# Two graph convolutions, part by products with the matrix of edges, part by gathered rows

## The chip, the cores and the metric

The kernel runs on one core of one Trainium2 chip. The metric is the device time of one execution in microseconds (us); the time of a kernel is the median of its runs. The engines are named as in the profile: PE is the matrix unit (PEld its weight load), DVE the vector engine, ACT the scalar engine, POOL the engine that issues gathers and scatters (indirect DMAs), SP the queue that issues the plain DMAs.

## The reference, cut to what matters

A network of eight layers works on 3125 nodes with 256 features and 53125 edges. The fifth layer is a pair of plain graph convolutions; the change concerns it.

```
deg  = segment_sum(1, dst);  dinv = rsqrt(deg);  norm = dinv[src] * dinv[dst]
def gcn_conv(h, W, b):
    m = (h @ W)[src] * norm[:, None]
    return segment_sum(m, dst) + b
x1 = gcn_conv(x, W1, b1)
x1 = x1 / max(norm of each row of x1, 1e-12)
x2 = gcn_conv(x1, W2, b2)
out = x2 + x
```

The edge list has one self loop per node besides (`src` and `dst` already hold one, the convolution adds a second). What costs is the sum over the edges of each node: row n of the result is the sum of the table's rows `src` over the edges that end in n.

## The kernel before, in words

**The nodes.** The nodes are put in order of falling number of edges and cut into `NT` = 25 groups of 128. Group g has `KS[g]` slots for edges, from 41 in group 0 to 10 in group 24; the last eight groups have 15, 15, 14, 14, 13, 12, 11 and 10 slots, 104 of the `TOT` = 453 in all. `OFF[g]` is where group g begins among them. A slot holds the number of the node at the other end of an edge (`recs_i[:, k, 0]`); slots beyond a node's edges are dead (`live` is 0 there, `pen` very negative).

**The layers that gather.** Most layers fetch one row per slot and node: `gather` (L1079) is one indirect DMA on POOL, 128 rows from a table in DRAM into one column of a tile; `scatter` (L1083) is the reverse. The relational convolution (`plain_sum`, 2153 to 2890 us in the profile) gathers 453 such columns of 128 x 256 numbers, four to a tile `gt`, and adds them on PE with an identity matrix (L1705).

**The matrix of edges.** The pair of plain convolutions doesn't gather. In the layer before it (a gate layer with experts, `gates_by_slots`, 2890 to 3790 us) the kernel builds, beside that layer's own gathers and matmuls, a matrix of edge counts `adj` in DRAM: for each group g a block of 128 x 25 x 128 numbers in bf16 (800 KB), which tells how many edges run from each of the 3200 nodes to each node of the group. `edge_places` works out the places, writes them to `slots_d`, and `edge_columns` loads them back in two DMAs for each group (L1774, L1777). `one_hots` makes two bf16 tiles on DVE (L1800), `edge_blocks` multiplies them on PE (L1813), ACT copies the product out (L1817, L1821), and SP stores it (L2494). `beside_gates` is a generator of 31 pieces: piece i makes the one-hots of group i - 3, the block of group i - 4, and a part of the experts' matmuls (`hidden` L2438, `back` L2452, `biased` L2459). The gate layer's loop `in_turns` takes pieces at a pace that follows its count of gathers. In that layer the order of the instructions on each engine is the order in which the program writes them.

**A convolution.** `edge_sum(table, tail)` runs twice. The nodes' rows times W, scaled by dinv, lie in a DRAM table (`tables[0]`, then `tables[1]`) and, for the self loop, in `own`. First five loads (L2556, 640 KB each) bring the table in, and ACT and DVE split it into three bf16 parts whose sum is the f32 value (`F12` and `F3_`, L2558 and L2559). Then, for each group: SP loads the group's block of `adj` (L2563, three buffers), PE multiplies it with the 25 tiles of the table, a matmul of 512 columns and one of 256 for each (L2566, L2569), so 50 matmuls a group into `acc` (two buffers in PSUM); DVE adds the halves and `own` (L2575, L2576); and a tail runs. `tail1` scales, and after every fifth group (`BATCH` = 5) normalises five groups, turns them on PE (L1454), multiplies by the second W (`to_table`, L2588), and scatters them into `tables[1]` (L1083), one step of that generator in each later turn of the group loop. `tail2` adds b2, the residual and the layer norm of the next layer, and the next layer's router matmul (L2643).

**What sets the order.** Here the program doesn't fix the order on each engine: a planner that works with its own costs for each instruction orders them when the kernel is built, by the program's order and by when it believes their inputs are there. It moves work that is ready ahead: in the profile the additions of b2 (L2628), which belong to the second convolution, run before the first.

Of the kernel before, what the change touches and what calls it, by code (L numbers as in the profile page):

```python
# [11 lines left out]
F32 = mybir.dt.float32  # L12
BF16 = mybir.dt.bfloat16
I32 = mybir.dt.int32
# [1040 lines left out]
DC = KS[0] + 3  # L1055
BATCH = 5
# [357 lines left out]
def quick(ctx: ExitStack, tc: tile.TileContext, a: dict, out: bass.AP, k):  # L1414
# [26 lines left out]
    def table_of(name, width, rows=NP + 1):  # L1441

        t = dram.tile([rows, width], F32, name=name)
        nc.sync.dma_start(t[NP : NP + 1, :], zero[:, :width])
        return t
# [266 lines left out]
    adj = dram.tile([NT, P, NT * P], BF16, name="adj")  # L1712
# [3 lines left out]
    for g in range(NT):  # L1716
        w = min(10, P // KS[g])
        n = -(-P // w)
        if at % P + n > P:
            at = -(-at // P) * P  # L1720
        TILES.append((w, n, at))
        at += n
    TB = -(-at // P)
    slots_d = dram.tile([2 * P * TOT], F32, name="slots_d")

    def slots_of(g):
        return slots_d[2 * P * OFF[g] : 2 * P * OFF[g + 1] if g + 1 < NT else 2 * P * TOT]

    t_at = q.tile([P, NT], F32, name="t_at")
    with tc.tile_pool(name="ep", bufs=1) as pool:  # L1730
        NJ = max(n for _, n, _ in TILES)
        firsts = pool.tile([P, NT, NJ], F32, name="ep_first")
        for g, (w, _, _) in enumerate(TILES):
            nc.gpsimd.iota(firsts[:, g, :], pattern=[[w, NJ]], base=w, channel_multiplier=0,
                           allow_small_or_imprecise_dtypes=True)
        j_f = pool.tile([P, 1], F32, name="ep_j")
        nc.gpsimd.iota(j_f, pattern=[[0, 1]], base=0, channel_multiplier=1, allow_small_or_imprecise_dtypes=True)
        past = pool.tile([P, NT, NJ], F32, name="ep_past")
        nc.vector.tensor_scalar(past, firsts, j_f, None, op0=ALU.is_le)
        t = t_at  # L1740
        nc.vector.tensor_reduce(t, past, AX.X, ALU.add)

        nc.vector.scalar_tensor_tensor(t, t, -1.0, firsts[:, :, 0], op0=ALU.mult, op1=ALU.mult)
        nc.vector.tensor_scalar(t, t, j_f, None, op0=ALU.add)

    def edge_places(pool):
# [12 lines left out]
        nc.vector.scalar_tensor_tensor(pb[:, 1, :], pen, -512.0 / BIG, pb[:, 1, :], op0=ALU.mult, op1=ALU.add)  # L1759
        for g in range(NT):  # L1760
            o = slice(OFF[g], OFF[g] + KS[g])
            nc.sync.dma_start(slots_of(g).rearrange("(s p k) -> p s k", s=2, p=P), pb[:, :, o])
# [650 lines left out]
    def beside_gates(pool, wp, psum):  # L2413
# [56 lines left out]
        for i in range(U + 3):  # L2470
# [6 lines left out]
            if 3 <= i < NT + 3:  # L2477
                hots[i - 3] = one_hots(pool, cols, columns, i - 3)
            g = i - 4
            products = iter(())  # L2480
            if 0 <= g < NT:
                As[g] = pool.tile([P, NT, P], BF16, name="em_a")
                products = edge_blocks(psum, g, *hots.pop(g), As[g])
# [9 lines left out]
            if 0 <= g - 1 < NT:  # L2493
                nc.sync.dma_start(adj[g - 1], As.pop(g - 1).rearrange("p b j -> p (b j)"))  # L2494
# [39 lines left out]
    with tc.tile_pool(name="ng", bufs=3) as gp, tc.tile_pool(name="ns", bufs=3) as sp, \  # L2534
# [10 lines left out]
        tables = [dram.tile([NP, D], F32, name=f"gcn{i}") for i in (1, 2)]  # L2545
# [4 lines left out]
        def edge_sum(table, tail):  # L2550
# [9 lines left out]
            tails = []  # L2560
            for g in range(NT):
# [3 lines left out]
                for b in range(NT):  # L2565
# [4 lines left out]
                                     skip_group_check=True)  # L2570
                for t in list(tails):
                    if next(t, None) is None:
                        tails.remove(t)
                s_ = sp.tile([P, D], F32, name="sum")
                nc.vector.tensor_add(s_, acc[:, 0, :], own[:, g, :])  # L2575
                nc.vector.tensor_add(s_, s_, acc[:, 1, :])  # L2576
# [20 lines left out]
        def tail1(g, acc):  # L2597
# [5 lines left out]
            sq = sp.tile([P, D], F32, name="sq")  # L2603
# [394 lines left out]
```

## Time and profile before

| what | us |
|---|---|
| median of 3 runs | 6321.4 (6282.28 to 6326.48) |
| the profiled execution, its own time | 6232.02 |
| its span | 6230.3 |
| gate layer, with the matrix of edges built beside it | about 2890 to 3790 |
| first convolution: first load of the table to its last scatter | 3903 to 4158 |
| second convolution: first load of the table to the last sum | 4159 to 4396 |

A view by stretches of time gives, for each stretch, how long each engine was busy and in brackets how many instructions it began, then the clock granted to PE (1.00 is full), the share of the 16 DMA engines and what they moved. A view by groups gives busy time and mean duration in ns of all instructions of a line, then the engine's idle time just before them and what ended it. "issue" means that the engine waited for nothing that the profile shows, "remote" that the releaser is not known. The mean PE clock over the span is 0.757.

### The profile page before, as it was taken

Reading aid. Unit: us, or ns where it says so; the run is one execution under the profiler, and the core shown is the slowest. Engines: PE = TensorE matmul, PEld = TensorE weight load, DVE = VectorE, ACT = ScalarE, POOL = GpSimd, SP = SyncE. Lnnn points to the kernel's source line nnn. Section 1 sums busy time; section 2 is a strip of 40 time slices with the busy share of each in tenths; the row PEclk is TensorE's granted clock in tenths of the full one; section 3 lists DMA queues with packets and bytes.
Section 4 is the critical chain, followed back from the end, with each engine's and each line's share of the span. In section 5 each row is a group of like instructions: output and inputs, shape, how many; then the busy total and the mean of one; then the engine's idle time right before and its main releaser. Section 6 shows DMA issues by size and latency. Waiting matters only on the chain. (4 is left out here: it accounts for less than half of the span.)

```text
span 6230.3 us, 45124 instructions
## 1 busy us (share of the span) xinstructions
PE 3790.6 (61%) x14119; PEld 2484.5 (40%) x14119; DVE 3125.4 (50%) x6023; ACT 1222.3 (20%) x2574; POOL 3127.8 (50%) x3044
## 2 busy tenths in 40 slices
PE   2345443455699854535396432889676788838882
PEld 1233332333455433423264221556343344436662
DVE  4588868898983345601164236333224677810001
ACT  1222222445622100000053221110121000012220
POOL 3677774677773266676467663010126666430004
PEclk9667666766799856756698666999656777869996
DMA  4534442333312233222252124332243333234442
GB/s 124 141 105 108 107 110 77 92 93 103 88 24 90 111 92 91 79 74 54 60 166 74 36 54 124 107 110 92 84 118 87 84 86 90 64 115 155 160 160 85
DMA packets 357953, 602.95 MB, mean 97 GB/s; under 512 B 109331, under 2 KB 254331, under 8 KB 354370
## 3 DMA queue, kind: packets, MB, share of 16 engines
q0 software_dynamic: 130800, 329.16, 20.1%
q1 hardware_dynamic: 207657, 251.79, 12.7%
q10 hardware_dynamic: 19238, 18.93, 1.0%
q8 instruction: 116, 1.90, 0.1%
q14 instruction: 142, 1.16, 0.1%
HBM read 458.77 MB, written 142.93 MB: 97 GB/s over the span
## 5 line engine op out<-in xcount | busy, mean ns | idle before, releaser
L1620 PE MATMUL acc<-wv,ident 128*128 128x256 f32 x2818 | 933.7, 492 | 611.9 <-ACT wv L1632 248.1
L1079 POOL DMA_INDIRECT gt<-T,recs x906 | 1011.3, 1116 | 341.4 <-issue 237.5
L1620 PEld LDWEIGHTS acc<-wv,ident 128*128 128x128 f32 x2818 | 666.6, 248 | 878.3 <-ACT wv L1632 280.1
L1079 POOL DMA_INDIRECT gt<-TA,recs x453 | 458.5, 1012 | 237.1 <-issue 124.8
L1079 POOL DMA_INDIRECT gt<-gm,recs x428 | 466.1, 1089 | 205.0 <-issue 126.8
L1079 POOL DMA_INDIRECT gt<-rel,relz x453 | 443.4, 979 | 203.6 <-issue 127.7
L1705 PE MATMUL acc<-gt,ident 128*128 128x256 f32 x906 | 321.9, 487 | 203.6 <-issue 155.7
L2566 PE MATMUL acc<-XNT,adj_g 128*128 128x512 bf16 x1250 | 416.4, 384 | 44.5 <-ACT XNT L2558 44.5
L2797 PE MATMUL e_ps<-EW,att 32*128 32x512 f32 (+7 forms) x466 | 300.5, 772 | 131.8 <-ACT att L2787 90.4
L1672 ACT ACTIVATE m<-m 128x1024 f32<-128x1024 f32 (+2 forms) x258 | 256.4, 994 | 614.0 <-DVE m L1671 378.2
L1671 DVE TENSOR_TENSOR m<-gt,R 128x1028 f32<-128x1028 f32 (+4 forms) x258 | 297.0, 1151 | 103.0 <-DMA gt<-T,recs 99.4
L1079 POOL DMA_INDIRECT y<-top_out,top_pos x50 | 48.0, 959 | 595.2 <-issue 594.9
L2569 PE MATMUL acc<-F,adj_g 128*128 128x256 bf16 x1250 | 342.8, 275 | 5.4 <-DVE F L2559 5.4
L1705 PEld LDWEIGHTS acc<-gt,ident 128*128 128x128 f32 x906 | 206.2, 240 | 301.7 <-issue 186.2
L1677 DVE TENSOR_TENSOR m<-m,att 128x1024 f32<-128x1024 f32 (+2 forms) x258 | 294.1, 1140 | 43.4 <-issue 28.1
L2909 PE MATMUL fh_ps<-xt,w 128*128 128x256 f32 x1024 | 265.1, 397 | 76.2 <-ACT ht L2911 75.4
L1678 DVE TENSOR_REDUCE L<-m 128x4 f32<-128x1024 f32 (+4 forms) x258 | 294.3, 1141 | 10.0 <-DVE m L1677 2.0
L1634 DVE TENSOR_TENSOR wv<-gt,L 128x1024 f32<-128x1024 f32 (+3 forms) x252 | 285.1, 1136 | 16.9 <-remote 12.8
L2438 PE MATMUL x_ps<-XNT,x_w 128*128 128x512 f32 (+1 forms) x448 | 213.2, 608 | 104.1 <-ACT x_h L2440 53.2
L2909 PEld LDWEIGHTS fh_ps<-xt,w 128*128 128x128 f32 x1024 | 186.6, 192 | 149.6 <-ACT ht L2911 127.8
L2452 PE MATMUL x_o<-x_w,x_h 128*128 128x256 f32 x800 | 204.5, 401 | 35.8 <-issue 32.9
L2921 PE MATMUL fo_ps<-w,ht 128*128 128x256 f32 x1024 | 226.3, 379 | 0.0
(557 smaller groups left out, 6417.9 us busy)
## 6 DMA issues: line engine op xcount, KB each, us to landing
w<-in_L_ffn_W_dram SPq DMA_DIRECT2D x64, 1024.0 KB
adj_g<-adj SPq DMA_DIRECT2D x50, 800.0 KB
adj<-em_a SPq DMA_DIRECT2D x25, 800.0 KB
gt<-T,recs POOLq DMA_INDIRECT x906
y<-each_d SPq DMA_DIRECT2D x25, 512.0 KB
each_d<-x_y SPq DMA_DIRECT2D x24, 512.0 KB
R<-rr SPq DMA_DIRECT2D x25, 388.0 KB
top_in<-zeros SPq DMA_DIRECT2D x8, 1024.0 KB
```

The source lines that it names most:

```text
L1079: return nc.gpsimd.indirect_dma_start(out=out_, out_offset=None, in_=table, in_offset=index(idx))
L1620: nc.tensor.matmul(acc, ident, wv[:, s, :], start=(c + s == 0), stop=(c + s == K - 1))
L1634: nc.vector.tensor_mul(wv[:, :n, :].rearrange("p s (h c) -> p s h c", h=H), t[:, :n, :D].rearrange("p s (h c) -> p s h c", h=H), L[:, c : ...
L1671: nc.vector.tensor_add(m[:, :n, :], st[g].tiles[c][:, :n, :], st[g].R[:, 1:2, :].to_broadcast([P, n, W]))
L1672: nc.scalar.activation(m[:, :n, :D], m[:, :n, :D], AF.Abs)
L1677: nc.vector.tensor_mul(m[:, :n, :D], m[:, :n, :D], att[:, None, :].to_broadcast([P, n, D]))
L1678: nc.vector.tensor_reduce(L, m[:, :n, :D].rearrange("p s (h c) -> p s h c", h=H), AX.X, ALU.add)
L1705: nc.tensor.matmul(accs[g], ident, t[:, s, :], start=False, stop=(last and s == n - 1))
L2566: nc.tensor.matmul(acc.rearrange("p s d -> p (s d)"), A[:, b, :], F12[:, b, :, :].rearrange("p s d -> p (s d)"), start=(b == 0), stop=Fals ...
L2569: nc.tensor.matmul(acc[:, 0, :], A[:, b, :], F3_[:, b, :], start=False, stop=(b == NT - 1), skip_group_check=True)
L2797: nc.tensor.matmul(e_ps[:, :z, :].rearrange("p s d -> p (s d)"), att, EW[: att.shape[0], s0 : s0 + z, :].rearrange("p s d -> p (s d)"), st ...
L2909: nc.tensor.matmul(ps[:, i, :], ld[j][1][:, c, (f_ + i) * P : (f_ + i + 1) * P], xt[j][:, c, :], start=(c == 0), stop=(c == KD - 1))
```

## The change

The matrix of edges is made and used for the first `GD` = 17 groups only. The other eight get their edge sums by gathers:

- `adj`, `slots_d`, `t_at`, `firsts` and `past` shrink to 17 groups; `edge_places`, `edge_columns`, `one_hots`, `edge_blocks` and the stores of `adj` run for 17.
- The two tables get one more row, of zeros, and a tile of indices `zi` points every dead slot of the last eight groups to it.
- In `edge_sum` a generator `gathered` gives, for each chunk of at most four slots (29 chunks, 104 gathers), the gathers into a tile `gt` (128 x 4 x 256, three buffers), one DVE reduction over the slots, and one DVE addition into `own`. Two chunks are taken after the products of each group. The gathers' order is groups 20 to 24, then 17 to 19.
- The groups' order is 0 to 9, 20 to 24, 10 to 19, so that a batch of five is either wholly products, wholly gathered, or (15 to 19) two of products and three gathered. A gathered group has no `acc`; its sum is `own` itself.
- The buffers of `sum` and `sq` go from three to two.

```diff
+GD = 17
-    adj = dram.tile([NT, P, NT * P], BF16, name="adj")
+    adj = dram.tile([GD, P, NT * P], BF16, name="adj")
-    for g in range(NT):
+    for g in range(GD):
         w = min(10, P // KS[g])
...
-    slots_d = dram.tile([2 * P * TOT], F32, name="slots_d")
+    slots_d = dram.tile([2 * P * OFF[GD]], F32, name="slots_d")
...
-        for g in range(NT):
+        for g in range(GD):
             o = slice(OFF[g], OFF[g] + KS[g])
             nc.sync.dma_start(slots_of(g).rearrange("(s p k) -> p s k", s=2, p=P), pb[:, :, o])
...
-            if 3 <= i < NT + 3:
+            if 3 <= i < GD + 3:
                 hots[i - 3] = one_hots(pool, cols, columns, i - 3)
             g = i - 4
             products = iter(())
-            if 0 <= g < NT:
+            if 0 <= g < GD:
                 As[g] = pool.tile([P, NT, P], BF16, name="em_a")
                 products = edge_blocks(psum, g, *hots.pop(g), As[g])
...
-            if 0 <= g - 1 < NT:
+            if 0 <= g - 1 < GD:
                 nc.sync.dma_start(adj[g - 1], As.pop(g - 1).rearrange("p b j -> p (b j)"))
...
-        tables = [dram.tile([NP, D], F32, name=f"gcn{i}") for i in (1, 2)]
+        tables = [table_of(f"gcn{i}", D) for i in (1, 2)]
+
+        o = OFF[GD]
+        z = wp.tile([P, TOT - o], F32, name="z_f")
+        nc.vector.tensor_scalar(z, recs_i[:, o:, 0], float(-NP), None, op0=ALU.add)
+        nc.vector.tensor_mul(z, z, live[:, o:])
+        zi = wp.tile([P, TOT - o], I32, name="z_i")
+        nc.vector.tensor_scalar(zi, z, float(NP), None, op0=ALU.add)
...
-            tails = []
-            for g in range(NT):
+            tails, ready = [], set()
+
+            def gathered():
+
+                for g in [*range(NT - BATCH, NT), *range(GD, NT - BATCH)]:
+                    for c, n in chunks(g):
+                        t = gp.tile([P, C4, D], F32, name="gt", bufs=3)
+                        for i in range(n):
+                            k_ = OFF[g] - OFF[GD] + c + i
+                            gather(nc, t[:, i, :], table, zi[:, k_ : k_ + 1])
+                        part = sp.tile([P, D], F32, name="g_part", bufs=2)
+                        nc.vector.tensor_reduce(part, t[:, :n, :].rearrange("p s d -> p d s"), AX.X, ALU.add)
+                        nc.vector.tensor_add(own[:, g, :], own[:, g, :], part)
+                        if c + n == KS[g]:
+                            ready.add(g)
+                        yield 0
+
+            def products(g):
                 A = gp.tile([P, NT, P], BF16, name="adj_g")
                 nc.sync.dma_start(A.rearrange("p b j -> p (b j)"), adj[g])
                 acc = psum.tile([P, 2, D], F32, name="acc", bufs=2)
...
+                return acc
+
+            beside = gathered()
+            for g in [*range(2 * BATCH), *range(NT - BATCH, NT), *range(2 * BATCH, NT - BATCH)]:
+                if g < GD:
+                    acc = products(g)
+                    for _ in range(2):
+                        next(beside, None)
+                while g >= GD and g not in ready:
+                    next(beside)
                 for t in list(tails):
                     if next(t, None) is None:
                         tails.remove(t)
-                s_ = sp.tile([P, D], F32, name="sum")
-                nc.vector.tensor_add(s_, acc[:, 0, :], own[:, g, :])
-                nc.vector.tensor_add(s_, s_, acc[:, 1, :])
+                s_ = own[:, g, :]
+                if g < GD:
+                    s_ = sp.tile([P, D], F32, name="sum", bufs=2)
+                    nc.vector.tensor_add(s_, acc[:, 0, :], own[:, g, :])
+                    nc.vector.tensor_add(s_, s_, acc[:, 1, :])
                 t = tail(g, s_)
...
-            sq = sp.tile([P, D], F32, name="sq")
+            sq = sp.tile([P, D], F32, name="sq", bufs=2)
```

## The prediction

> **What bounds the kernel now.** I read the stages first: the view by stretches over the two convolutions, from the first sums to the last.
>
> ```profile
> 3927.00:4144.00 217.00, 213.87 (x1305) 133.67 (x1304) 65.24 (x168) 16.24 (x41) 18.55 (x17) 1.00 0.31 104
> 4183.00:4396.00 213.00, 209.38 (x1310) 129.03 (x1308) 63.41 (x191) 10.01 (x26) 0.00 (x0) 0.99 0.26 87
> ```
>
> The columns are PE, PEld, DVE, ACT, POOL, then PE clock, DMA share, GB/s. PE works without a break at full clock, DVE for 30%, POOL hardly at all. So here PE is the bound, and each group's products are on the path. Their price comes from the timeline of DVE, by the distance between sums.
>
> ```profile
> 3954.21 0.42 DVE L2575 TENSOR_TENSOR sum<-acc,own 128x256 f32<-128x256 f32 x1 [5.81 <-PE acc L2569]
> 3962.33 0.42 DVE L2575 TENSOR_TENSOR sum<-acc,own 128x256 f32<-128x256 f32 x1 [5.81 <-PE acc L2569]
> ...
> 4051.39 0.42 DVE L2575 TENSOR_TENSOR sum<-acc,own 128x256 f32<-128x256 f32 x1 [6.90 <-PE acc L2569]
> 4060.60 0.42 DVE L2575 TENSOR_TENSOR sum<-acc,own 128x256 f32<-128x256 f32 x1 [3.95 <-PE acc L2569]
> ```
>
> A group costs 8.12 us on PE (50 matmuls); with a step of a tail (4 matmuls of L2588, 2 of L1454) 9.21. DVE waits some 6 us of each for PE.
>
> The new work is gathers beside matmuls, so I looked where the kernel does that already: the relational convolution, first the instructions that touch the tile `gt`, then a burst of gathers by stretches of 5 us.
>
> ```profile
> L1079 POOL DMA_INDIRECT gt<-rel,relz x450: 943/949/2987, 2153.2 to 2867.1; - x150
> ```
>
> ```profile
> 2284.00:2289.00 5.00, 5.00 (x24) 4.43 (x23) 1.42 (x5) 0.00 (x0) 3.78 (x5) 0.99 0.38 105
> 2289.00:2294.00 5.00, 5.00 (x25) 4.37 (x23) 4.76 (x11) 0.00 (x0) 3.78 (x5) 1.00 0.38 104
> 2294.00:2299.00 5.00, 1.86 (x5) 0.62 (x3) 4.83 (x10) 0.00 (x0) 3.78 (x5) 0.88 0.35 105
> ...
> 2304.00:2309.00 5.00, 1.17 (x2) 0.57 (x2) 2.52 (x6) 0.00 (x0) 3.78 (x5) 0.50 0.37 104
> 2309.00:2314.00 5.00, 1.17 (x2) 0.47 (x2) 0.00 (x0) 0.00 (x0) 3.78 (x5) 0.50 0.37 105
> ```
>
> This is the finding on which the forecast turns. A gather takes 0.95 us of POOL, and the timeline shows 0.30 between two: 1.25 us. The burst starts at 2281; PE begins 24 matmuls in 5 us, then, some 14 us into the burst, only 2, with its clock at 0.50, though DMA moves no more than before. It stays so until POOL stops. A second burst (from 2327) shows the same after 17 us. I call this the drag: POOL issues gathers without a pause for 14 to 17 us (I take 16, 13 gathers), and the other engines almost stop. When POOL pauses they come back, 3.5 us after the end of the last issue (2485.2 to 2488.7) or 5.5 (2535.7 to 2541.1). The profile gives no cause ("issue").
>
> The stage that builds the matrix of edges has the same, and waits:
>
> ```profile
> POOL gt L1079 <- DVE pen L2342: 67.6, 2, 34.6
> POOL own L1079 <- DVE L L2343: 53.8, 1, 53.8
> ```
>
> There POOL's gathers are the bound for most of the time, broken by waits for DVE, which has queued behind PE.
>
> **What the Trainium skill says.** "DMA: Bandwidth & Descriptors", section "Issuing engines are not separate DMA queues": DMAs from POOL and SP interleave on the same 16 engines. The trace agrees that they can: loads for `adj` and gathers together would be 98 GB/s (800 KB in 8.12 us) plus 105 GB/s, and the stretch 3800 to 3850 moved 276 at a share of 0.87; so transfers fit. "SBUF — State Buffer", section "Who interferes with whom": a tensor_reduce never contends with POOL on this chip, a DVE instruction with two SBUF inputs contends with what POOL reads there. In the trace gathers beside the one-hots (L1800, two SBUF inputs) stretch from 0.95 to 2.2 and 3.1 us. So the new reductions shouldn't slow the gathers; the one-hots taken away did. "TensorE: Matmul & The Clock Gate", part 1: after an idle window of about 3.4 us the array runs at half clock, and as long a busy time lifts it; the clock of 0.50 above agrees. No page describes the drag.
>
> **The change, part by part.**
>
> *Products removed.* 8 groups x 8.12 = 65.0 us of PE for each convolution; the tails of these groups stay. 17 x 8.12 + 25 x 1.09 = 165 stays of 230.
>
> *Gathers added.* 104 x 1.25 = 130 us of POOL for each convolution, beside 165 of PE. The first twelve (three tiles) can run while the table is loaded (9 us from the first load to the first matmul, over 20 to the last split): covered. Then two chunks a group: the first ten groups take 72 gathers, 7.2 each, 9.0 us, against 9.2 of PE. So without the drag they are just hidden; POOL hardly ever pauses, and the drag comes. Over two groups: 14.4 gathers, 18.0 us; PE has done 16.0 of its 18.4, 2.4 is left. POOL then stops, since its three tiles wait for reductions that stand on DVE behind the sum of the group PE hasn't finished. PE returns after 4, and needs 2.4 at full or 4.8 at half clock, say 3.4: 25.4 in place of 18.4, a loss of 7.0. First convolution: (72 - 12) / 14.4 = 4.2 such cycles, 29 us; its last 32 gathers share POOL with the scatters of `tail1`, before each of which POOL waits now (8.12 us each time, for ACT), and these pauses break the bursts: nothing. Second convolution: no scatters, 92 / 14.4 = 6.4 cycles, 45 us.
>
> *Reductions and additions on DVE.* 29 per convolution. The shape isn't in the trace. L1678 reduces 1024 numbers in 1.22 us; L2356, which reads with a stride as the new one will, takes 0.72 for about 350, so 2.1 for 1024 at most. With 0.42 for the addition two chunks cost 3.3 to 5.0 us a group, beside 2.6 that DVE does now (65.24 / 25): 7.6 at most of 9.2, hidden under PE. If PE's cover were gone it would be 48 to 73 us.
>
> *Ends.* Groups 17 to 19 come last with no products, so the last batch's scaling, square and reduction (0.48 + 0.42 + 0.42 each) no longer lie beside matmuls: 3 x 1.3 = 4, with a step of the earlier tails about 5 us for each convolution (0 to 12).
>
> *The matrix for 17 groups.* One-hots, 61 of 252 copies on ACT, 8 stores and 16 loads of `em_w` go. The first group concerned is met at 3389 us. From there to 3780 POOL issues for about 291 us, its gathers are stretched by one-hots of the groups removed by 3.4 + 3.1 + 4.2 + 3.6 + 3.9 = 18 us (excess over 0.95), and it waits 33 and 22 us for DVE, during which pieces take 15.4 us each (stores of `adj` at 3550.9, 3566.1, 3582.2), of which the 15 or 16 edge matmuls at 0.17 are 2.7: three pieces, 8 us. The 16 loads on SP (0.7 to 1.5 us each, up to 2960) may let PE start earlier: 5. Against it: the stretched gathers were pauses that ended the drag, and without them bursts are longer; I take off 11. Sum 20, between -15 and +45.
>
> *Nothing:* `z`, `zi`, the row of zeros, fewer stores of `slots_d`: a handful of small instructions beside the layer before, under 2 us if uncovered. `sum` and `sq` with two buffers: both are used up within 1.4 us on DVE itself.
>
> *Sum.* First convolution 65 - 29 - 5 = 31, second 65 - 45 - 5 = 15, gate layer 20: 66. The profiled execution, 6232 (its span 6230.3 and 1.7 around it), would become 6166. It lay 1.4% below the median of the runs shown, so I take the difference from the median: 6321.4 - 66 = 6255.
>
> **Rivals.**
>
> *The gathers are hidden.* Waits of POOL on DVE, or stretched gathers, break the bursts before 16 us, and the drag never sets in. For it: in the gate layer's stretch 3150 to 3250, where one-hots break the bursts, PE is busy for 89 of 100 us. Against it: 14.4 gathers in 18 us leave no pause. Gain 2 x (65 - 5) + 20 = 140: 6181.
>
> *The planner runs the gathers ahead.* If by its costs a gather is cheaper than it is, more chunks' reductions stand on DVE ahead of each sum than the two of the program. With three: 12 gathers, 15 us, and some 2 until the tiles are free again; 104 / 12 = 8.7 groups at 17 and 8.3 at 9.2 are 224 us, and with the ends nothing is gained: 20 - 10 = 10, 6311. For it: the additions of b2 show how far it moves work ahead.
>
> *Slower.* The same mechanism, past that point of three chunks a group: if all reductions stand ahead of the first sums, nothing on DVE holds POOL back, the burst lasts 130 us, and PE does 16 us of work in it, then comes back after 4 and does 149: 283 against 230. Two such are 2 x (53 + 5) - 20 = 96 lost: 6417. Against it: three tiles only, and the program's order.
>
> **How the numbers follow.** The likeliest case, drag in part, has 0.45, its own range 6205 to 6300 (drag after 14 or 17.5 us, gate layer at its bounds); hidden 0.2; three chunks ahead 0.2; slower 0.15. About 1% (63 us) is what a measurement of this kernel can tell from no change. Faster by more: a little over half of the first case, all of the second, a little of the third, 0.49. Slower: most of the fourth, 0.14. The same: 0.37. The range, 6165 to 6385, takes in the second case and leaves out most of the fourth.
>
> **What would show it.** Right: PE's instructions drop in stretches of 5 us after 13 gathers in a row, a period of two groups near 25 us in the second convolution, and the first gaining more than the second. Wrong: groups at 8.1 to 9.2 us throughout (hidden), or a run of more than 20 gathers with PE at x2 (slower). If the gate layer's end moves by more than 45 us either way, my account of that stage is wrong.

## The result, and the profile after

| | before | changed |
|---|---|---|
| median of 14 runs, us | 6306.22 (6269.32 to 6330.69) | 6347.26 (6308.49 to 6376.61) |
| profiled execution, span | 6230.3 | 6308.6 |
| first convolution, first split of the table to the next convolution's first split | 255.6 | 277.6 |
| of it, to the first sum | 27.5 | 52.8 |
| second convolution, first split to last sum | 231.0 | 249.4 |
| of it, to the first sum | 28.1 | 54.1 |
| gate layer, first gather of rows of `gm` to the last reduction | 860.6 | 859.6 |

The changed kernel takes 1.0069 times as long (95% interval 1.0048 to 1.0090), 0.7% more, where 1% less was forecast. The two profiles differ by 78 us, and 40 of them lie in the two convolutions. Most of the rest is 22 us ahead of the gate layer, where the change touches almost nothing, and 20 us behind the second convolution. Profiles of one kernel differ there by as much: the changed kernel begins its gate layer at 2903.7 us in one profile (e9) and at 2960.6 in another (e17), and from the last sum on the kernel before takes 1834.8 us here and 1848.3 in e12. So these 42 us aren't put down to the change. Line numbers of the changed kernel are 2 higher than before from L1057 to L1758, and 3 to 38 higher after that (L2575 became L2613).

The stretches of the convolutions, from first sums to last, answer to the two shown of before (217 us with PE busy for 213.87, 213 with 209.38).

```profile
3979.00:4070.00 91.00, 45.92 (x199) 22.00 (x204) 41.99 (x63) 0.21 (x1) 56.70 (x60) 0.68 0.38 113
4070.00:4175.00 105.00, 104.21 (x622) 66.65 (x633) 40.49 (x115) 11.24 (x32) 15.46 (x15) 1.00 0.31 107
4258.00:4352.00 94.00, 44.66 (x195) 20.89 (x200) 43.53 (x69) 0.21 (x1) 56.96 (x60) 0.67 0.38 111
4352.00:4453.00 101.00, 99.64 (x628) 63.00 (x640) 38.50 (x137) 5.61 (x18) 0.00 (x0) 1.00 0.22 74
```

Each convolution falls in two. While POOL gathers, PE is busy for half the time. Then no gathers are left, and PE runs the other groups at full clock with no gathers beside them. By the program's order the gathers were to lie beside 15 of the 17 groups; they lie beside the first six.

The reason is seen in the order in which DVE's instructions were built. Here r is a reduction of a chunk, f a split of the table (L2569), S the sum of a group:

```
first convolution   rfrfffrrrffffrrrfrfrrSSrrrrSrrrrSrrrrrSrrrrrSSSSSSSSSSSS
```

The program asks for two reductions a group. The planner put 11 of the 29 ahead of the first sum, none ahead of the second, 4 or 5 ahead of each of the next four, and several ahead of the splits, on which the first products wait. The timeline of DVE shows what that costs at the start:

```profile
3924.64 1.88 DVE L2581 TENSOR_REDUCE g_part<-gt 128x256 f32<-128x1024 f32 x1 [25.30 <-DMA gt<-gcn,z_i]
3926.45 1.48 DVE L2569 TENSOR_TENSOR F<-F,XNT 128x1280 f32<-128x1280 f32 x1
...
3930.60 1.89 DVE L2581 TENSOR_REDUCE g_part<-gt 128x256 f32<-128x1024 f32 x1 [2.34 <-DMA gt<-gcn,z_i]
3932.41 4.30 DVE L2569 TENSOR_TENSOR F<-F,XNT 128x1280 f32<-128x1280 f32 x3
...
3969.20 1.90 DVE L2581 TENSOR_REDUCE g_part<-gt 128x256 f32<-128x1024 f32 x1 [2.77 <-DMA gt<-gcn,z_i]
3977.44 1.88 DVE L2581 TENSOR_REDUCE g_part<-gt 128x256 f32<-128x1024 f32 x1 [6.34 <-DMA gt<-gcn,z_i]
3979.24 0.42 DVE L2613 TENSOR_TENSOR sum<-acc,own 128x256 f32<-128x256 f32 x1
```

A split stands behind a reduction that waits for its gathers, again and again. And the first sum stands behind the eleventh reduction. PE had finished both groups for which it has buffers at 3972.2, and stood still until the sums freed them:

```profile
3980.47 0.58 PE L2592 MATMUL acc<-XNT,adj_g 128*128 128x512 bf16 x1 [8.28 <-DVE sum L2613]
```

The drag of the prediction is there too: PE almost stops while POOL issues gathers. Below this is also called starving. By stretches of 5 us of the changed kernel (columns as before):

```profile
3985.00:3990.00 5.00, 5.00 (x30) 2.89 (x29) 3.85 (x5) 0.00 (x0) 3.78 (x5) 0.93 0.38 106
3990.00:3995.00 5.00, 0.99 (x5) 0.19 (x2) 1.69 (x2) 0.00 (x0) 3.78 (x5) 1.00 0.37 102
3995.00:4000.00 5.00, 0.96 (x2) 0.20 (x2) 0.63 (x1) 0.00 (x0) 3.78 (x5) 0.60 0.37 98
4000.00:4005.00 5.00, 0.95 (x2) 0.21 (x2) 0.00 (x0) 0.00 (x0) 3.07 (x4) 0.50 0.46 114
4005.00:4010.00 5.00, 2.35 (x6) 0.97 (x8) 0.44 (x2) 0.00 (x0) 0.00 (x0) 0.50 0.05 16
```

PE begins 2 matmuls in 5 us with no wait in its timeline but "issue". POOL's last issue ends at 4003.98, and the sum of PE's group starts at 4009.56, 5.6 us later. The gathers themselves went nearly as fast as thought (0.95 us in the median; the mean of 1.02 comes from those beside the splits, up to 2.5):

```profile
L1081 POOL DMA_INDIRECT gt<-gcn,z_i x208 | 211.5, 1017 | 101.3 <-issue 63.6 <-DVE g_part L2581 36.2 <-DMA gt<-gcn,z_i 1.2
```

In the gate layer two of POOL's waits are nearly those of before (61.4 for `pen` and 52.7 for `L`, where before has 67.6 and 53.8). A third, for `gates_o`, is longer (before, then changed):

```profile
POOL gd L1083 <- DVE gates_o L2365: 40.3, 2, 21.8
```

```profile
POOL gd L1085 <- DVE gates_o L2368: 76.5, 4, 31.8
```

### The profile page after: what moved, and what is told of

Same layout as the page of the kernel before. It is cut to its first block, busy times and chain, and to the rows that moved or that the text cites. A ratio compares the mean times of both kernels' runs of the same rounds, so it can differ in the third digit from the quotient of the medians.

```text
span 6308.6 us, 43526 instructions
## 1 busy us (share of the span) xinstructions
PE 3676.1 (58%) x13164; PEld 2400.3 (38%) x13201; DVE 3170.2 (50%) x6086; ACT 1194.4 (19%) x2512; POOL 3330.6 (53%) x3244
## 5 line engine op out<-in xcount | busy, mean ns | idle before, releaser
L1622 PE MATMUL acc<-wv,ident 128*128 128x256 f32 x2818 | 919.9, 487 | 608.0 <-ACT wv L1634 285.5
L1707 PE MATMUL acc<-gt,ident 128*128 128x256 f32 x906 | 321.0, 484 | 209.0 <-issue 159.4
L2592 PE MATMUL acc<-XNT,adj_g 128*128 128x512 bf16 x813 | 296.4, 409 | 130.6 <-ACT XNT L2568 64.0
L2595 PE MATMUL acc<-F,adj_g 128*128 128x256 bf16 x850 | 244.1, 288 | 63.3 <-issue 40.0
L1081 POOL DMA_INDIRECT gt<-gcn,z_i x208 | 211.5, 1017 | 101.3 <-issue 63.6
L2462 DVE TENSOR_TENSOR x_y<-x_o,x_b 128x512 f32<-128x512 f32 (+1 forms) x52 | 34.5, 669 | 411.2 <-remote 242.7
```

The source lines that it names most:

```text
L1081: return nc.gpsimd.indirect_dma_start(out=out_, out_offset=None, in_=table, in_offset=index(idx))
L1622: nc.tensor.matmul(acc, ident, wv[:, s, :], start=(c + s == 0), stop=(c + s == K - 1))
L1707: nc.tensor.matmul(accs[g], ident, t[:, s, :], start=False, stop=(last and s == n - 1))
L2592: nc.tensor.matmul(acc.rearrange("p s d -> p (s d)"), A[:, b, :], F12[:, b, :, :].rearrange("p s d -> p (s d)"), start=(b == 0), stop=Fals ...
L2595: nc.tensor.matmul(acc[:, 0, :], A[:, b, :], F3_[:, b, :], start=False, stop=(b == NT - 1), skip_group_check=True)
```

## The experiments

The runs fell into two sorts. In the first (the result, e1 to e4, e9 to e12, e16, e17) the kernel before takes 6209 to 6306 us and gathers starve PE as above. In the second (e5 to e8, e13 to e15, e18) it takes 5855 to 5863, and PE works on beside gathers. What makes the sort isn't known. Kernels that ran together on one chip fell in one sort, but number 6 of the chips stands on record with e1 to e4 in the first and with e18 in the second; whether that is one and the same chip, the record doesn't say. Times of whole kernels are compared within one sort only. The convolutions of the kernel before, which have no gathers, take the same in both, so theirs may be compared across.

"Second" in the table ends at the last sum by products. Behind it the last router matmul of the layer ends 12 to 13 us later (before, changed, e3, e11), in e5 19 us later.

| run | split to first sum, 1st and 2nd | first convolution | second | ratio to before (95%) |
|---|---|---|---|---|
| **first sort** | | | | |
| e12 before | 27.7, 27.4 | 255.7 | 230.3 | |
| e9 changed | 53.1, 61.4 | 276.4 | 248.5 | 1.0100 (1.0069 to 1.0132) |
| e17 changed | 51.2, 62.6 | 278.3 | 251.1 | 1.0094 (1.0062 to 1.0127) |
| e1 program's order | 35.2, 34.0 | 276.8 | 251.1 | 1.0122 (1.0059 to 1.0184) |
| e2 before, program's order | 29.0, 28.0 | 275.6 | 264.5 | 1.0070 (1.0042 to 1.0099) |
| e3 no gathers | 28.5, 26.9 | 193.1 | 161.9 | 0.9816 (0.9759 to 0.9872) |
| e4 quarter rows | 54.9, 55.6 | 283.6 | 250.9 | one run |
| e11 two behind each sum | 29.0, 28.0 | 246.3 | 211.9 | 1.0000 (0.9980 to 1.0020) |
| e10 one chunk a group | 28.9, 29.0 | 243.5 | 209.0 | 0.9983 (0.9959 to 1.0007) |
| e16 matrix of 17 only | 28.4, 27.6 | 256.2 | 230.4 | 1.0028 (1.0002 to 1.0055) |
| **second sort** | | | | |
| e15 before | 27.2, 27.7 | 255.2 | 230.5 | |
| e7 late start | 26.9, 26.9 | 260.9 | 228.6 | one run |
| e8 splits first | 32.1, 30.4 | 258.6 | 225.2 | one run |
| e5 one chunk a group | 29.3, 28.5 | 198.5 | 164.8 | 0.9734 (0.9718 to 0.9751) |
| e6, e14, e18: 20 groups | 27 to 31 | 217 to 218 | 196 | 0.9828, 0.9826, 0.9835 (each ±0.002) |
| e13 matrix of 17 only | 26.5, 28.5 | 254.4 | 231.3 | 0.9921 (0.9908 to 0.9935) |

**e1 and e2: the program's order, and its control.**

```diff
-            beside = gathered()
-            for g in [*range(2 * BATCH), *range(NT - BATCH, NT), *range(2 * BATCH, NT - BATCH)]:
+            with tc.manual_schedule():
+                beside = gathered()
+                for g in [*range(2 * BATCH), *range(NT - BATCH, NT), *range(2 * BATCH, NT - BATCH)]:
```

(e2: the same around the loop of the kernel before. Both have a tiny instruction on POOL between scatters.)

> The changed kernel, but the loop over groups in both convolutions keeps the program's order on each engine (two chunks of gathers a group). In the changed kernel the planner put 11 of 29 reductions ahead of the first sum on DVE and 4 to 5 ahead of each of the next, and each convolution took 22 us longer than before (277.7 against 255.7 from first load to the next convolution's first load; 258.7 against 236.8 from first load to last sum). Theory 'order': two chunks a group break the bursts of gathers, so the forecast of the prediction holds: first convolution 225 (213 to 237), second 222 (210 to 234), the whole about 80 to 90 us under the changed kernel. Rival 'drag in any order': 13 gathers in a row starve PE whoever orders them: both convolutions within 8 us of 278 and 259. Rival 'start only': what is lost is the late first sum (62 us after the first load against 33): 29 us less each, 249 and 230, with the groups after it no faster.

> The kernel before with the same edit (program's order in the loop over groups): the control for the run above. Every theory: PE is the bound of these loops and has its 8.12 us a group in either order, so 255 and 237 within 6 us each, and the time within 0.3% of before. If it loses or gains more, that much of the other run's difference is the order itself and not the gathers.

Without its control e1 would have been misread: it looks like "drag in any order". But e2 lost 20 and 34 us with no gather in it (against e12). Its sums lie up to 13.5 us apart; that the steps of the tails stand badly in the program's order is read from this and not tested. Against the control, e1's convolutions are 1 us longer and 13 shorter. The edit is too blunt; e11 replaces it.

**e3 and e4: no gathers, and short ones.** In e3 the calls of `gathered` are taken out. In e4:

```diff
-                            gather(nc, t[:, i, :], table, zi[:, k_ : k_ + 1])
+                            gather(nc, t[:, i, :64], table.rearrange("n (q d) -> (n q) d", q=4), zi[:, k_ : k_ + 1])
```

> The changed kernel without the gathers, reductions and their additions in the two convolutions: the last eight groups get only their self loop (their edge sums are left out). It prices all that the gathers cost. Convolutions: 255.7 - 65 = 191 and 236.8 - 65 = 172, within 8 us, for every theory. Gate layer with the matrix of 17 groups (first gather of that layer to its last reduction, 860.6 before and 859.6 in the changed kernel): theory 'the matrix was hidden there': 855 to 865 again, so the whole gains 2 x 65 = 130 us, 6175; theory of the prediction (20 us less, hidden in the profile by chance): about 840, the whole 6155.

> The changed kernel with each gather fetching 64 numbers in place of 256 (the sums of the last eight groups are taken over wrong, shorter rows); the same number of gathers, in nearly the same order, a quarter of the bytes. Theory 'the bytes starve PE': convolutions 200 to 225 and 185 to 215, PE at its 15 matmuls in 2.5 us through the bursts. Theory 'the issuing starves PE': PE still falls to 1 or 2 in 2.5 us, convolutions within 10 us of 278 and 259 (reductions are shorter by 4 x, but they waited for gathers, not for DVE).

e3 gives the floor: 65 us less a convolution was rightly reckoned (62.6 and 68.4 against e12). So 104 gathers cost 83 to 87 us (e9 less e3) in the planner's order, more than the products they replace. e4 is clear on the bytes: at a quarter of them PE still begins 2 matmuls in 5 us while POOL issues.

```profile
4000.00:4005.00 5.00, 0.96 (x2) 0.10 (x1) 0.81 (x2) 0.00 (x0) 3.78 (x5) 0.50 0.15 26
4005.00:4010.00 5.00, 0.96 (x2) 0.21 (x2) 0.00 (x0) 0.00 (x0) 3.78 (x5) 0.50 0.15 26
```

26 GB/s in place of 100, and PE no faster: the bytes don't do it. e4 left the number of gathers and of their rows (128 each) as it was, so whether the issuing starves PE or the number of rows isn't told apart. The Trainium skill, "SBUF — State Buffer", section "Who interferes with whom", says that PE never waits on anyone; it speaks of the ports of SBUF. In these runs PE stands still beside gathers. What it waits on no view shows, so it isn't shown that the ports are what holds it.

**e5 to e8: pacing, and the start.** e5 (e6 with `GD` = 20 and chunks of four):

```diff
-                        t = gp.tile([P, C4, D], F32, name="gt", bufs=3)
+                        t = gp.tile([P, 7, D], F32, name="gt", bufs=2)
...
+                        with tc.issue_after(turn.sum):
-                        nc.vector.tensor_reduce(part, t[:, :n, :].rearrange("p s d -> p d s"), AX.X, ALU.add)
+                            nc.vector.tensor_reduce(part, t[:, :n, :].rearrange("p s d -> p d s"), AX.X, ALU.add)
...
-                    nc.vector.tensor_add(s_, s_, acc[:, 1, :])
+                    turn.sum = nc.vector.tensor_add(s_, s_, acc[:, 1, :]).ins
```

A group's slots are cut into even chunks, and the chunks are taken behind the sum of the group and no longer ahead of it: one a group, a second one after group 10 (e6: after the first two groups). `issue_after` only fixes the place on DVE, behind the sum; the rest stays the planner's. e7 makes the indices from the last split (`F3_` times 0 plus index), e8 queues all reductions behind the last split.

> The changed kernel with the planner's order, but one chunk of at most seven gathers a group (two buffers in place of three), and each reduction queued on DVE behind the sum of its group. POOL can then issue at most 14 gathers at the start and 5 to 7 after each sum, and waits in between. Without any gathers the two convolutions took 193.1 (first split of the table to the next convolution's first split) and 161.9 (first split to last sum), with the gathers of the changed kernel 277.6 and 249.4: 0.82 us for each gather. Theory 'long bursts': PE is starved only by more than some 13 gathers in a row, so pauses cure it: 193 to 212 and 162 to 182, the time 1 to 1.7% under before. Rival 'each gather costs PE its share': 278 and 249 again, within 10. Between the two: a part of the drag needs no long burst.

> As the run above with 20 groups by products and five (60 gathers) by rows, chunks of at most four, one a group. POOL then has 3 to 4 gathers, 4 to 5 us, in each turn of 8 to 9 us, and rests for half of it. Without gathers 20 groups would take 193.1 + 3 x 9.2 = 221 and 161.9 + 3 x 9 = 189. Theory 'long bursts': within 10 us of that, 221 to 231 and 189 to 199, the time 0.8 to 1.1% under before. Rival 'each gather costs PE its share', 60 x 0.82 = 49 more: 270 and 238, the time no better than before.

> The changed kernel, but the indices of the gathers are made from the last split of the table, so that no gather starts before the table is split; the planner's order otherwise. In the changed kernel the first sum came 53 us after the first split (before: 27.5). Theory 'the gathers hold up the start': first sum 27 to 30 us after the first split, and the rest as it was: 252 and 225. Rival 'drag': the first sum comes as early, but the 25 or so gathers that had run at the start now run beside the products and cost there what they cost before: both convolutions within 8 us of 278 and 249.

> The changed kernel with all reductions queued on DVE behind the last split of the table; gathers start as early as before, but stop after three tiles, until the splits are done. Theory 'DVE's order held up the splits' (each split stood behind a reduction that waits for its gathers): first sum 28 to 34 us after the first split in place of 53. Rival 'gathers slow the loads, the copies and the first products themselves': 40 us or more. The rest of each convolution has 3 to 5 reductions ahead of each sum and drags as in the changed kernel: whole convolutions 255 to 270 and 227 to 242.

These were runs of the second sort, so they don't test what pauses do against starving. The view by stretches of e5 shows it at once: 30 gathers on end from 3655.8, and PE stays at 32 matmuls in 5 us (first sort: 2).

```profile
3665.00:3670.00 5.00, 4.95 (x32) 3.05 (x32) 3.41 (x3) 0.00 (x0) 3.78 (x5) 1.00 0.41 130
3675.00:3680.00 5.00, 4.95 (x31) 3.03 (x31) 4.76 (x6) 0.00 (x0) 3.78 (x5) 1.00 0.59 184
3680.00:3685.00 5.00, 5.00 (x33) 3.03 (x31) 2.26 (x3) 0.00 (x0) 3.78 (x5) 1.00 0.57 195
```

And they show the planner's order alone. In e7, where the first sum is as early as in the kernel before and PE isn't starved, the convolutions gain nothing all the same (260.9 and 228.6), while those of e5 come within 5.4 and 2.9 us of the floor of e3. DVE of e7, one group:

```profile
3678.54 0.42 DVE L2617 TENSOR_TENSOR sum<-acc,own 128x256 f32<-128x256 f32 x1
...
3679.33 1.90 DVE L2585 TENSOR_REDUCE g_part<-gt 128x256 f32<-128x1024 f32 x1
...
3684.16 1.91 DVE L2585 TENSOR_REDUCE g_part<-gt 128x256 f32<-128x1024 f32 x1 [1.88 <-DMA gt<-gcn,z_t]
...
3688.81 1.93 DVE L2585 TENSOR_REDUCE g_part<-gt 128x256 f32<-128x1024 f32 x1 [2.07 <-DMA gt<-gcn,z_t]
...
3695.55 1.88 DVE L2585 TENSOR_REDUCE g_part<-gt 128x256 f32<-128x1024 f32 x1 [4.36 <-DMA gt<-gcn,z_t]
...
3699.36 0.41 DVE L2617 TENSOR_TENSOR sum<-acc,own 128x256 f32<-128x256 f32 x1
```

Sums are 20.8 us apart, the time of the gathers that stand between them. PE needs 8.1 and then waits for a sum with both `acc` full (8.55 and 9.85 us at 3679.6 and 3700.6). e8's first sum at 32 and 30 us answers for DVE's order as the cause of the late start, but in this sort of run, in which the changed kernel itself wasn't run.

**e9 to e12: changed, before and paced in runs of the first sort.** e10 is the kernel of e5. e11 is its edit with the chunks of four, the three buffers and the two chunks a group of the changed kernel.

> The changed kernel itself, beside the paced one, since the chips differ: the kernel before took 6306 us where the result was taken, 6217 with the first four experiments, 5857 with the next four, and in these last PE ran its matmuls at 15 in 2.5 us beside gathers without a break, which it didn't on the other two. Theory 'order' (the planner puts 4 to 5 chunks of gathers ahead of each of the first sums, so these groups last as long as the gathers, 130 us, and the other eleven follow alone at 9.2): the convolutions take some 260 and 228 even where PE isn't starved, and 278 and 249 where it is. Rival 'starving only': where PE isn't starved the convolutions take 200 and 170.

> One chunk of at most seven gathers a group, each reduction behind its group's sum, as before (198.5 and 164.8 us there, on a chip that starves PE little). Theory 'order': the same 195 to 205 and 160 to 170 on any chip, 60 to 80 us a convolution under the changed kernel beside it. Rival 'pauses don't cure starving': on a chip that starves PE 225 or more and 195 or more. If the chip is of the second sort this run only repeats the other.

> The chunks, the three buffers and the two chunks a group of the changed kernel, with the planner's order but for one thing: each reduction is queued on DVE behind the sum of its group. This is the case that the prediction took for the likeliest, in which POOL hardly pauses. The prediction's number for it: first convolution 31 us less than before (about 225), second 15 less (about 222, from first load to last sum; 216 from first split), with two groups in 25 us. Theory 'order, and no starving': groups 10 to 11 us apart for 15 groups (8 gathers at 1.25), 215 and 180. Theory 'starving in long bursts' on a chip that does it: 225 to 245 and 205 to 230.

> The kernel before on the same chip as the three above, for its stages. Convolutions 250 to 256 and 228 to 231 on every chip (PE is the bound and has no gathers beside it). Gate layer 855 to 862 where gathers starve PE, 710 to 725 where they don't, with the matrix of 25 groups as with that of 17: then the matrix costs nothing there on either.

This set separates the two causes on one chip. From e9 to e11 the reductions move behind their sums, and with them the place in the program from which the chunks are taken; nothing else differs: 30.1 and 36.6 us. Of these 24.1 and 33.4 are the start (first sum at 29.0 and 28.0 in place of 53.1 and 61.4). In e11 all splits and the first sum stand ahead of the first reduction, and the sum waits for PE alone:

```profile
3929.46 1.49 DVE L2569 TENSOR_TENSOR F<-F,XNT 128x1280 bf16<-128x1280 f32 x1 [1.32 <-ACT XNT L2568]
3932.62 0.42 DVE L2612 TENSOR_TENSOR sum<-acc,own 128x256 f32<-128x256 f32 x1 [1.66 <-PE acc L2596]
...
3933.41 1.92 DVE L2582 TENSOR_REDUCE g_part<-gt 128x256 f32<-128x1024 f32 x1
```

Behind the first sum e11 is hardly better than e9 (217 and 184 us against 223 and 187). e10 and e5 are the same kernel in the two sorts of run: 45.0 and 44.2 us in the convolutions, nearly all behind the first sum, which is what starving costs that kernel. What it costs the changed kernel in its own order wasn't measured apart.

Did the pauses of e10 not help, or were there none? By its timeline the first three sums lie 5.0 and 5.7 us apart, each lets 5 to 7 gathers go, and so 19 follow one another from 3941.9 on. Through these (first three lines) PE holds for 14.6 us, some 12 gathers, and then starves. A burst of 6 (a scatter and 5 gathers) with rests of 5.0 and 2.7 us around it (4078.5 to 4086.1) leaves it alone (last two):

```profile
3950.00:3955.00 5.00, 5.00 (x32) 3.02 (x31) 2.36 (x1) 0.00 (x0) 3.78 (x5) 1.00 0.58 204
3955.00:3960.00 5.00, 2.09 (x9) 0.59 (x7) 1.92 (x5) 0.00 (x0) 3.78 (x5) 1.00 0.35 100
3960.00:3965.00 5.00, 1.89 (x5) 0.34 (x4) 0.00 (x0) 0.00 (x0) 3.78 (x5) 0.52 0.37 107
```

```profile
4078.50:4083.50 5.00, 5.00 (x29) 2.86 (x28) 2.79 (x5) 0.14 (x1) 3.80 (x4) 0.88 0.57 212
4083.50:4088.50 5.00, 5.00 (x32) 3.28 (x30) 1.23 (x3) 0.48 (x2) 1.96 (x3) 1.00 0.44 100
```

So do three bursts of 5 gathers with rests of 2.8 and 2.9 us in the second convolution (4256.9 to 4280.8), in which PE begins 33 matmuls in 5 us.

The long bursts of e1, e10 and e11 behave as this one does: behind the first sum of their first convolutions there are 15 bursts of 11 or more, and in 14 of them PE falls off 12.4 to 15.2 us after the first issue, with 75 to 90 matmuls begun. The changed kernel shows that this isn't a rule of time alone: its first 64 gathers follow one another from 3917.7 on, while PE stops again and again for splits and sums, and PE falls off only at 3990.3, 72.6 us after the first issue, 43 matmuls after its last stop. What resets or sets off the starving stays open.

So my pacing failed to pace. The numbers of the rival of e10 came (225 or more and 195 or more; 243.5 and 209.0), but the pauses that it was to judge weren't there.

The expectation for e12's gate layer missed (828.0 us where 855 to 862 was said). That led to the last question.

**e13 to e18: the gate layer, and shorter bursts.** e13 and e16 are the kernel before with the matrix of 17 groups and

```diff
-                nc.sync.dma_start(A.rearrange("p b j -> p (b j)"), adj[g])
+                nc.sync.dma_start(A.rearrange("p b j -> p (b j)"), adj[min(g, GD - 1)])
```

> The kernel before, with the matrix of edges built for 17 groups only; its convolutions multiply the block of group 16 again in place of the blocks of the last eight groups (these groups' sums are wrong), so PE does the same work there. This is the part of the change in the gate layer alone. Medians so far say two things: where gathers starve PE, the three kernels with a matrix of 17 groups took about 17 to 23 us more than their convolutions explain; where they don't, the two took some 30 us less. The prediction: 20 us gained (between -15 and +45). Theory 'the gate layer is bound by the gathers and their starving, and shorter stretching means longer bursts': on a starving chip +5 to +30 us, ratio 1.001 to 1.005, on the other -20 to -40 us, 0.993 to 0.997. Rival 'hidden everywhere': within 5 us, ratio 0.999 to 1.001, and what the medians say comes from elsewhere.

> 20 groups by products, five by gathers of at most four a group, as before (217.6 and 195.9 us on a chip that starves PE little). On a starving chip, theory 'a gather costs PE a share however short its burst': the runs with 104 gathers and pauses took 243.5 and 209 there, 45 us over the other chip, 0.43 us for each gather; 60 gathers are 26 more, 244 and 222. Theory 'only bursts of some ten or more': bursts of 4 with pauses of 4 us cost nothing but at the start (14 gathers beside the first products): 220 to 230 and 196 to 206.

> The kernel before once more, for its stages on this chip: convolutions 255 to 256 and 230 to 231; gate layer 828 to 861 on a starving chip (the three profiles so far: 860.6, 856.4, 828.0; with 17 groups six profiles lay within 854 to 860), about 715 to 750 on the other. If it lies under 850 on a starving chip again, the matrix of 17 groups lengthened that layer.

> The part of the change in the gate layer alone once more (the convolutions multiply block 16 again for the last eight groups). On a chip that starves PE little it took 42 us off (ratio 0.992; gate layer 712.5 us against 743.9). On a starving chip, theory 'longer bursts': 5 to 30 us more than before, ratio 1.001 to 1.005. Rival 'hidden': 0.999 to 1.001. Rival 'less work is less work': 0.992 again. On a chip of the other sort it repeats 0.992.

> The changed kernel beside it. On a starving chip: as twice before, ratio 1.005 to 1.013, convolutions 276 to 278 and 248 to 250. On the other, theory 'order': convolutions some 260 and 228 (six groups as long as the gathers, eleven alone) against 255 and 230.5 before, nothing gained in them, and the 42 us of the gate layer are all that is left: ratio 0.990 to 0.995. Rival 'starving only': 200 and 170 there, ratio 0.974.

> 20 groups by products, five by gathers of at most four a group with rests between, for a chip that starves PE (on one that doesn't: 217.6 and 195.9 us, 218.1 and 196.4). Theory 'a gather costs PE its share however short its burst' (0.43 us each, from the runs with 104 paced gathers): 244 and 222. Theory 'only bursts of some ten or more': the start costs some, the rest nothing: 220 to 230 and 196 to 206, and the time under before by 0.5% or more. On a chip of the other sort it repeats 218 and 196.

The smaller matrix gains 0.79% in the second sort (46 us of 5863; 31 us in the layer by the profiles, 743.9 to 712.5) and loses 0.28% in the first (18 us of 6273, between 1 and 35). POOL's groups of lines show where: e15 and e13, then e12 and e16.

```profile
L1079 POOL DMA_INDIRECT gt<-gm,recs x428 | 513.4, 1199 | 138.6 <-issue 116.8 <-DMA gt<-gm,recs 8.3 <-DVE L L2349 5.0
```

```profile
L1081 POOL DMA_INDIRECT gt<-gm,recs x428 | 485.8, 1135 | 137.2 <-issue 116.4 <-DMA gt<-gm,recs 9.1 <-DVE L L2352 5.2
```

```profile
L1079 POOL DMA_INDIRECT gt<-gm,recs x428 | 478.2, 1117 | 190.0 <-issue 127.3 <-DVE pen L2342 49.3 <-DMA recs<-csr_d,PR 6.4
L1083 POOL DMA_INDIRECT gd<-gates_o,own_at x25 | 24.8, 991 | 31.4 <-DVE gates_o L2365 24.4 <-issue 5.5 <-DMA recs<-csr_d,PR 0.9
```

```profile
L1081 POOL DMA_INDIRECT gt<-gm,recs x428 | 444.0, 1037 | 206.7 <-issue 127.6 <-DVE pen L2345 73.9 <-DMA gt<-gm,recs 4.0
L1085 POOL DMA_INDIRECT gd<-gates_o,own_at x25 | 26.8, 1073 | 123.2 <-DVE gates_o L2368 117.1 <-issue 6.1
```

In both sorts the gathers get shorter without the one-hots, by 28 and 34 us. In the second sort POOL keeps it. In the first it comes back, and more, as waits for DVE (`gates_o` 24.4 to 117.1, `pen` 49.3 to 73.9).

The pair of the first sort lies at the two ends of what is on record, so its size is no measure: the gate layer takes 828.0 us in e12 and 896.5 in e16, but 856.4 (e2) and 860.6 in the other two profiles with the matrix of 25 groups, and 854.1 to 866.2 in the other eight with that of 17. Over all of them two things hold. The gathers are shorter with 17 groups (444 to 461 us busy against 466 to 478), and the waits for `gates_o` are longer (64 to 117 us against 24 to 63). The waits for `pen` overlap (60 to 74 against 35 to 68). That DVE is late there because PE is starved for longer I infer from the convolutions; no run took it apart.

e14 and e18 met the second sort again (217 to 218 and 196 us, at the floor of 221 and some 7 over that of 189), so a kernel that really keeps its bursts short was not run in the first sort; that it would gain there is read from e10's short burst, not shown. e17 repeats the result.

## Why the prediction was wrong

**The sum against what came**, for the result's two profiles, and e16 for the gate layer. First convolution: 31 gained was forecast, 22.0 were lost, of them 25.3 before the first sum. Second: 15 forecast, 18.4 lost, 26.0 of them before the first sum. Gate layer: 20 forecast, 18 lost. So 66 gained became 58 lost, or 0.92%. With the interval of e16 (1 to 35 us in place of 18) the sum is 41 to 75 us, 0.7 to 1.2%. The result's medians say 0.69%, those of e17 and e9 0.94% and 1.00%.

**The step that failed first** is "The first twelve (three tiles) can run while the table is loaded: ... covered." The gathers ran there, but their reductions stood on DVE ahead of the splits and of the first sum. I had priced the reductions as busy time (1.89 us measured, 2.1 at most forecast: right) and never as waits with the splits queued behind them. e11, which takes the reductions behind their sums, brings the first sum back to 28 to 29 us and takes 30.1 and 36.6 us off, so this step is shown.

**"Then two chunks a group"** took the program's order for DVE's. The rival "The planner runs the gathers ahead" and the slower rival with its turning point of three chunks a group described what happened: 11, then 4 to 5. I gave them 0.35 together and the program's order 0.45, though the only evidence on the planner, the additions of b2, spoke for them. Their price was not met either: 6417 for all reductions ahead was too much, since not all stood ahead, and three tiles and DVE's waits did stop POOL for 8.75 us at 4004.

**The drag** was read rightly for the case of the prediction, two chunks a group behind each other (its onset is 12.4 to 15.2 us, 10 to 12 gathers, in these loops, where I took 16 and 13). In the first sort of run a period of 25 to 28 us for two groups stands in e11 (19.2 and 9.1, 17.0 and 8.1, 13.8 and 11.5), and its second convolution gained 18.4 against e12, where the prediction had 15. Its first gained 9.4, not 31, so the second gained more than the first and not less. There "these pauses break the bursts: nothing" was wrong: behind the tenth group, where gathers share POOL with scatters, e11's sums lie 22.8, 9.2, 17.6 and 11.0 apart where e3 has 15.4, 9.2, 9.2 and 9.2, 17.6 us more. The test "a run of more than 20 gathers with PE at x2 (slower)" came true. That the transfers fit together was right: e10 moved 204 GB/s in the stretch at 3950, with gathers in it and loads for `adj` under way. The stretch at 3800 from which the prediction took this has no gathers in it.

**Gate layer.** The term of the one-hots was 18 us. The gathers got shorter by 28 in the second sort and by 5 to 34 in the first, depending on the profiles: the direction was right. The layer as a whole moved the other way in the first sort. There something took back all of it and some 18 us more. In the prediction's sum this belongs to "longer bursts", "I take off 11"; that it is longer bursts isn't shown, only that the time comes back as waits for DVE. The prediction's own test here, an end moved by more than 45 us, didn't come (860.6 and 859.6).

**The ends**, 5 us a convolution: from the last sum of the first convolution to the next split, e3 takes 25 us and e12 21, so 4 us: right. In the second the last router matmul ends 1 us later. But the prediction left out another gap. Groups 20 to 24 take their turn after group 9, with their tails and no products, and there e3 has one distance between sums of 15.4 and of 12.6 us where 9.2 and 8.1 lie otherwise: 6 and 4 us more.

So two causes are shown. DVE's order lost the start, and it is enough to leave the convolutions without a gain where nothing starves (e7). Starving costs 44 to 45 us a convolution where the order is mended (e10 against e5). With the order mended and PE starving, e11's convolutions gain 28 us together, and the whole kernel gains nothing (1.0000). Without both, e5 is 2.7% faster than before in the second sort, 0.8% of it by the smaller matrix alone (e13). In the first sort, e10 is not to be told from before, and 1.2% faster than the changed kernel beside it (0.9983 against 1.0100). The change as it stands wasn't run in the second sort.

## What to carry to other kernels

An instruction that waits for a gather costs what is queued behind it on its engine, so look up where the built order puts it, not where the program writes it, and pin it behind the work that must not wait. Before gathers are put beside matmuls, find out from a stage that already has both how long PE holds through a burst in the runs at hand (mostly 12 to 15 us in one sort here, through 30 gathers and more in the other), and keep the bursts shorter by what releases them; that this last step gains was not run here. And a control for an edit of the order (e2) is cheap against the wrong conclusion that it saves. Last, one pair of profiles can mislead about a stage (828 and 896 us in the gate layer): look at all profiles of a kernel before a difference is explained.

## What the runs showed of the hardware

- Two sorts of run, with one kernel: 6209 to 6306 us against 5855 to 5863. The convolutions without gathers take the same in both (255.7 and 255.2, 230.3 and 230.5); stages with gathers beside other work differ (the gate layer 828 to 861 against 744).
- In the first sort PE begins 2 matmuls in 5 us while POOL issues gathers, at 100 GB/s as at 26; it comes back 5.6 us after the end of the last issue (4003.98 to 4009.56). In the second it kept 32 through 30 gathers on end.
- In the first sort the onset lies mostly 12.4 to 15.2 us after a burst's first issue (14 of 15 bursts of e1, e10 and e11), but 72.6 us after it where PE stopped for other things between (the changed kernel). In one case each, a rest of 0.7 us between two bursts didn't start the count anew (e11 at 4024), and one of 2.7 us did (e10 at 4088). What PE waits on isn't shown.
